# Two graph-attention layers on sparse neighbour lists: one release per tile, the last tiles of layer 0 placed earlier, another order of layer 1's tiles

## The chip, the cores and the metric

The kernel runs on one core of a Trainium2 chip, as one launch. The metric is the device time of that launch in microseconds; the median of several runs is given, and one further execution was taken with the profiler.

## What is computed

The input x is (8, 2048, 256), the adjacency matrix (2048, 2048) holds very few ones in a row. Cut to what matters:

```python
# layer 0: attention over the neighbours, a softmax in each chunk of 256 columns
scores = clip(einsum('bhnd,bhjcd->bhnjc', q, kc) / sqrt(Dh), -10, 10)
scores = where(mask == 0, -10, scores)
attn   = softmax(scores, axis=-1)
out    = einsum('bhnjc,bhjcd->bhnd', attn, vc) @ Wo.T + bo + x
x1     = layernorm(x + layernorm(out) * gamma + beta)
# layer 1: graph attention on x1, softmax over the neighbours
Wh     = x1 @ W
alpha  = softmax(where(mask, leaky_relu(s_src[:, :, None] + s_dst[:, None]), -inf), axis=2)
y      = layernorm(x1 + elu(einsum('bijh,bjhd->bihd', alpha, Wh)))
```

## The kernel before

**Tiles.** The kernel first turns the adjacency matrix into neighbour lists and sorts the 2048 nodes by their number of neighbours. 128 nodes make a tile, so there are 16 tiles, and `CAPS` (L34) gives the most neighbours that a node of each has: 24, 14, 13, 12, 11, 11, 10, 10, 9, 9, 8, 8, 7, 7, 6, 5. A "row" below is one neighbour of each of a tile's 128 nodes. The 8 batches are taken two at a time as four groups in layer 0 (`G` = 2, `NG` = 4) and four at a time as two halves in layer 1. Layer 0 therefore works through 4 x 16 = 64 tiles, layer 1 through 2 x 16 = 32.

**Gathers and the ring.** For each row, `gather` (L469) issues one indirect DMA on GpSimd's queue (L475), which fetches 128 table rows of 4 KB, from `kv_d` for layer 0 and from `wh_d` for layer 1. They land in a ring of 14 units of two rows each (`RING`, L39). A unit is free again once TensorE has summed its rows (`summed`, L500). VectorE multiplies the rows by weights beforehand (`weighted`, L487), and ScalarE does a part of them (L493). Before that, layer 0 multiplies by the queries (L533, L540), sums the products on TensorE (L552) and forms a softmax (L582 is its exponential); layer 1's softmax is in `softmax1` (L679 is its exponential).

**Layer 0's end of a tile.** `finish0` (L615) multiplies the context by Wo (L621), adds the input (L627), normalizes twice (L631 to L636), and stores the result in `x1_d`. `rows1` (L639) then multiplies that result by W (L649) and stores a block of 128 rows of `wh_d` (L653). A gather of layer 1 may read any row of its half's `wh_d`, so the first gather of a half needs the last block of that half.

**Layer 1's end of a tile.** `context1` (L689) ends with the load of `xr`, the tile's own rows of layer 0's result, on SP's queue (L711); `xr` has two buffers. `finish1` (L714) transposes the sums (L720), forms the ELU and adds `xr` (L724, L727), normalizes, and puts a scatter on the list `late`. The scatter goes out on GpSimd's queue. In the second half it writes four blocks straight to the output (L739), back in the nodes' own order. In the first half it writes to a table `hold_d` in that order (L734), and `release` (L760) later copies the held rows from there to the output, DRAM to DRAM, on SP's queue (L764), four transfers of 128 KB per tile.

**The order of the work.** It is written out by hand in `seq` (L750 to L758): groups 0 and 1 of layer 0 alone, then pairs of layer 0's tiles in groups 2 and 3 with one tile of layer 1's first half between the two of each pair, three pairs behind (`lag`), then layer 1's second half alone. `order` (L748) gives the tile for each place, for both layers alike: 15, 13, 11, ... 1, 0, 2, ... 14. In a pass of the loop, `fetch` (L777) first issues the gathers of the next place, then `scatters` sends what is in `late`. A tile of layer 1 that stands between two of layer 0 is only noted (`waiting`), and its context is formed in the next pass. The second half's passes, and those of the first half's last three tiles, run the last branch (L816 to L825): `softmax1`, `finish1` of the place before, from the third tile of the second half on one `release`, then `context1`. The two passes after layer 0's last tile also hold what is left of layer 0: `rows1` of tile 62 and `finish0` of tile 63 in the first, `rows1` of tile 63 in the second, in each case after `finish1` and before `context1`. A scheduler of the programming layer makes each engine's order out of this: it may move an instruction ahead of others of its engine where dependences allow.

Of the kernel before, what the change touches and what calls it, by code (L numbers as in the profile page):

```python
# [17 lines left out]
P = 128  # L18
# [15 lines left out]
CAPS = (24, 14, 13, 12, 11, 11, 10, 10, 9, 9, 8, 8, 7, 7, 6, 5)  # L34
TOP = 24
REC = 32
G = 2
# [134 lines left out]
def sparse_path(ctx: ExitStack, tc: tile.TileContext, keep, x, adj, Wq, bq, Wk, bk, Wv, bv, Wo, bo, gamma, beta, W, a,  # L172
                out):
    nc = tc.nc
    B, N, F = x.shape
    KC = F // P
    NT = N // P
    NCH = N // CH
    NG = B // G
# [13 lines left out]
    hold_d = [nc.dram_tensor(f"hold_d{p}", [N, 2 * GF], F32).ap() for p in range(NG // 2 - 1)]  # L193
# [313 lines left out]
    out_v = dram_disjoint_views(orows, 2 * NT * B)  # L507
# [150 lines left out]
    def fetch1(p, t):  # L658
        got1[p, t] = gather(2 * WW, wh_d[p], idx1, t)

    def softmax1(p, t):
        S = CAPS[t]
        units = got1[p, t]
        z = small.tile([P, 2, GH, S], F32, tag="z1", name="z1")
        for u, s0, n in units:
            nc.vector.tensor_tensor(z[:, :, :, s0:s0 + n].rearrange("p k e s -> p s k e"),
                                    u.rearrange("p s (k w) -> p s k w", k=2)[:, :, :, GF:GF + GH],
                                    sd[p % 2][:, t].unsqueeze(1).to_broadcast([P, n, 2, GH]), op=ALU.add)
        z = z.rearrange("p k e s -> p (k e) s")
        nc.vector.scalar_tensor_tensor(z, z, SLOPE, z, op0=ALU.mult, op1=ALU.max)  # L670

        neg = small.tile([P, S], F32, tag="neg", name="neg")
        nc.vector.tensor_scalar(neg, valid[:, t, 0:S], -1.0, 1e30, op0=ALU.add, op1=ALU.mult)
        nc.vector.tensor_tensor(z, z, neg.unsqueeze(1).to_broadcast([P, 2 * GH, S]), op=ALU.add)
        m = small.tile([P, 2 * GH], F32, tag="m", name="m")
        nc.vector.tensor_reduce(m, z, axis=AX.X, op=ALU.max)
        nc.vector.tensor_tensor(z, z, m.unsqueeze(2).to_broadcast([P, 2 * GH, S]), op=ALU.subtract)
        e = z
        nc.scalar.activation(e, z, AF.Exp)  # L679
        nc.vector.tensor_tensor(e, e, valid[:, t, 0:S].unsqueeze(1).to_broadcast([P, 2 * GH, S]), op=ALU.mult)  # L680
        r = small.tile([P, 2 * GH], F32, tag="r", name="r")
        nc.vector.tensor_reduce(r, e, axis=AX.X, op=ALU.add)

        nc.vector.tensor_scalar(r, r, 1e-30, None, op0=ALU.max)
        nc.vector.reciprocal(r, r)
        nc.vector.tensor_tensor(e, e, r.unsqueeze(2).to_broadcast([P, 2 * GH, S]), op=ALU.mult)  # L686
        st1[p, t] = e
# [61 lines left out]
    lag = 3  # L749
    seq = [(0, i) for i in range(2 * NT)]  # L750
# [6 lines left out]
            seq.append((0, 2 * NT + 2 * j + 1))  # L757
    seq += [(1, NT + j) for j in range(NT)]  # L758

    def release(p, t):  # L760

        for b in range(p * 2 * G, (p + 1) * 2 * G):
            c = b - p * 2 * G
            nc.sync.dma_start(out_v[NT * B + t * B + b][b * N + t * P:b * N + (t + 1) * P, :],  # L764
                              hold_d[p][t * P:(t + 1) * P, c * F:(c + 1) * F])

    def scatters():
        for f in late:
# [3 lines left out]
    def at(i):  # L772
        return i // NT, order[i % NT]

    fetched = [0]

    def fetch(k):  # L777

        while fetched[0] <= min(k, len(seq) - 1):
            layer, i = seq[fetched[0]]  # L780
            (fetch1 if layer else fetch0)(*at(i))
            fetched[0] += 1

    fetch(0)
    waiting = None
    for k, (layer, i) in enumerate(seq):
        g, t = at(i)
        between = layer == 0 and seq[k + 1][0] == 1
        tables_first = layer == 0 and seq[k + 1][0] == 0 and seq[k + 1][1] % NT == 0
        if not tables_first:  # L790
            fetch(k + 1)
        scatters()
        if layer == 0:
            scores0(g, t)
            if between and i + 1 < NG * NT:
                softmax1(*at(seq[k + 1][1]))
            if waiting is not None:

                if waiting:
                    finish1(*at(waiting - 1))  # L800
                context1(*at(waiting))
                waiting = None
            if i > 1:
                rows1(*at(i - 2))
            if i:
                finish0(*at(i - 1))
            if g + 1 < NG:
                tables(g + 1, i % NT)
            if tables_first:
                fetch(k + 1)  # L810
            softmax0(g, t)
            context0(g, t)
        elif seq[k - 1][0] == 0 and seq[k - 1][1] + 1 < NG * NT:
            waiting = i
        else:
            softmax1(g, t)  # L816
            finish1(*at(i - 1))
            if i >= NT + 2:
                release(g - 1, i - NT - 2)
            if seq[k - 1] == (0, NG * NT - 1):  # L820
                rows1(*at(NG * NT - 2))
                finish0(*at(NG * NT - 1))
            if seq[k - 2] == (0, NG * NT - 1):
                rows1(*at(NG * NT - 1))
            context1(g, t)  # L825
    scatters()
    finish1(*at(NG // 2 * NT - 1))
    scatters()
    for t in range(NT - 2, NT):
        for p in range(NG // 2 - 1):  # L830
# [429 lines left out]
```

## Time and profile before

| | |
|---|---|
| median of 6 runs | 2439.85 us |
| lowest and highest | 2431.14 and 2450.51 us |
| the profiled execution | 2445.62 us |
| its span, first to last instruction | 2443.9 us |
| PE, PEld busy | 1884.6 us (77%), 1615.9 us (66%) |
| DVE, ACT, POOL busy | 1843.0 us (75%), 1402.2 us (57%), 1479.3 us (61%) |
| gathers L475 from `kv_d` | 656, mean 1228 ns |
| gathers L475 from `wh_d` | 328, mean 1223 ns |
| releases on SP's queue | 64, 128 KB each, 8.2 us in the median from issue to landing |
| loads of `xr` | 32, 512 KB each, 5.2 us in the median from issue to landing |

PE is TensorE's matrix multiplication, PEld its loading of weights, DVE VectorE, ACT ScalarE, POOL GpSimd, SP SyncE, which here only issues DMAs. [...] The instructions that issue DMAs on SP are not counted as busy time; on POOL the indirect ones are. "L475" is a line of the kernel above. In a timeline, the bracket at the end of a line gives the time the engine stood idle before the instruction, and the event that came last before it started.

### The profile page before, as it was taken

Reading aid. Unit: us, or ns where it says so; the run is one execution under the profiler, and the core shown is the slowest. Engines: PE = TensorE matmul, PEld = TensorE weight load, DVE = VectorE, ACT = ScalarE, POOL = GpSimd, SP = SyncE. Lnnn points to the kernel's source line nnn. Section 1 sums busy time; section 2 is a strip of 40 time slices with the busy share of each in tenths; the row PEclk is TensorE's granted clock in tenths of the full one; section 3 lists DMA queues with packets and bytes.
Section 4 is the critical chain, followed back from the end, with each engine's and each line's share of the span. In section 5 each row is a group of like instructions: output and inputs, shape, how many; then the busy total and the mean of one; then the engine's idle time right before and its main releaser. Section 6 shows DMA issues by size and latency. Waiting matters only on the chain. (4 is left out here: it accounts for less than half of the span.)

```text
span 2443.9 us, 38937 instructions
## 1 busy us (share of the span) xinstructions
PE 1884.6 (77%) x11946; PEld 1615.9 (66%) x11946; DVE 1843.0 (75%) x4095; ACT 1402.2 (57%) x5031; POOL 1479.3 (61%) x1225
## 2 busy tenths in 40 slices
PE   6687787688988889999899997875767775455764
PEld 5565676577767778777788786764756664444653
DVE  4874467877767788867889887887879886656775
ACT  4573354355655566555566675666455577556766
POOL 1114644676545558376578757776778753758874
PEclk9998888889999999999999998987979987778887
DMA  6754886688888779598879979996779975986873
GB/s 218 253 189 142 299 286 224 223 305 321 284 290 289 260 239 378 206 362 310 285 265 346 354 259 337 325 305 231 232 234 328 363 271 173 379 286 228 288 277 109
DMA packets 240750, 669.11 MB, mean 274 GB/s; under 512 B 44455, under 2 KB 70826, under 8 KB 238486
## 3 DMA queue, kind: packets, MB, share of 16 engines
q0 software_dynamic: 156800, 505.01, 59.2%
q1 hardware_dynamic: 80016, 151.56, 17.0%
q10 hardware_dynamic: 3718, 9.97, 1.3%
q8 instruction: 98, 1.61, 0.3%
q14 instruction: 118, 0.97, 0.1%
HBM read 612.79 MB, written 126.36 MB: 302 GB/s over the span
## 5 line engine op out<-in xcount | busy, mean ns | idle before, releaser
L475 POOL DMA_INDIRECT u<-kv_d,idx x656 | 805.3, 1228 | 429.4 <-PE acc L500 165.1
L500 PE MATMUL acc<-ident,u 128*128 128x128 f32 x5248 | 726.1, 294 | 204.1 <-DVE u L487 130.1
L500 PEld LDWEIGHTS acc<-ident,u 128*128 128x128 f32 x5248 | 646.6, 153 | 268.8 <-DVE u L487 178.2
L475 POOL DMA_INDIRECT u<-wh_d,idx x328 | 401.3, 1223 | 155.6 <-issue 68.3
L552 PE MATMUL pr<-ident,u 128*128 128x128 f32 (+1 forms) x1984 | 283.9, 293 | 78.3 <-DVE u L533 63.4
L487 DVE TENSOR_TENSOR u<-u,al 128x1024 f32<-128x1024 f32 x280 | 332.5, 1221 | 1.3
L533 DVE TENSOR_TENSOR u<-u,qx 128x1024 f32<-128x1024 f32 (+1 forms) x248 | 295.3, 1191 | 27.7 <-DMA u<-kv_d,idx 24.5
L487 DVE TENSOR_TENSOR u<-u,z 128x1024 f32<-128x1024 f32 x266 | 315.1, 1213 | 0.8
L552 PEld LDWEIGHTS pr<-ident,u 128*128 128x128 f32 (+1 forms) x1984 | 244.0, 150 | 108.1 <-DVE u L533 86.1
L493 ACT ACTIVATE u<-u,z 128x64 f32<-128x64 f32 x1008 | 261.0, 336 | 27.8 <-DVE z L686 18.4
L493 ACT ACTIVATE u<-u,al 128x64 f32<-128x64 f32 x800 | 210.7, 342 | 42.4 <-DVE al L593 41.6
L348 POOL TENSOR_TENSOR xt<-xt,beta_r 128x1024 f32<-128x1024 f32 x32 | 80.1, 2507 | 186.1 <-PE tk L334 157.1
L382 PE MATMUL tk<-wq,xT 128*128 128x256 f32 x512 | 150.4, 410 | 44.6 <-ACT kvs L376 44.6
L649 PE MATMUL mf<-wa,x1T 128*128 128x264 f32 x512 | 157.8, 434 | 20.5 <-ACT x1T L644 10.5
L369 PE MATMUL tk<-wkv,xT 128*128 128x256 f32 x512 | 146.1, 399 | 14.9 <-ACT xC L339 14.7
L621 PE MATMUL mf<-wo,cT 128*128 128x256 f32 x512 | 143.8, 404 | 9.9 <-ACT whs L652 9.1
L540 DVE TENSOR_TENSOR u<-u,qx 128x1024 f32<-128x1024 f32 (+1 forms) x96 | 110.4, 1153 | 47.2 <-DMA qx<-qx_d,node 24.0
L373 PE MATMUL tk<-wkv,xC 128*128 128x256 f32 x512 | 143.5, 397 | 0.0
L649 PEld LDWEIGHTS mf<-wa,x1T 128*128 128x128 f32 x512 | 97.2, 207 | 54.8 <-ACT whs L652 23.0
L382 PEld LDWEIGHTS tk<-wq,xT 128*128 128x128 f32 x512 | 94.4, 205 | 58.5 <-ACT kvs L376 49.5
L441 ACT ACTIVATE sq<-o,nm 128x256 bf16<-128x256 f32 x256 | 129.4, 506 | 5.0
L437 ACT ACTIVATE nm<-sums 128x2 f32<-128x2 f32 (+1 forms) x160 | 32.4, 202 | 161.8 <-DVE sums L627 85.6
(166 smaller groups left out, 3160.7 us busy)
## 6 DMA issues: line engine op xcount, KB each, us to landing
kv_d<-kvs SPq DMA_DIRECT2D x48, 512.0 KB, 6.5
wh_d<-whs SPq DMA_DIRECT2D x64, 260.0 KB, 4.6
xt<-in_x_dram SPq DMA_DIRECT2D x64, 256.0 KB, 4.1
qx_d<-xt SPq DMA_DIRECT2D x32, 512.0 KB, 3.3
qx_d<-qs SPq DMA_DIRECT2D x64, 256.0 KB, 6.0
x_d<-o SPq DMA_DIRECT2D x64, 256.0 KB, 5.3
xr<-x_d SPq DMA_DIRECT2D x32, 512.0 KB, 5.2
u<-kv_d,idx POOLq DMA_INDIRECT x656, 6.3
```

The costliest lines, as they stand in the source:

```text
L369: nc.tensor.matmul(pm[:, 0:F], xT[:, b * KC + kc, rows], wkv[:, kc, 0:F], start=(kc == 0), stop=False, skip_group_check=True)
L373: nc.tensor.matmul(pm[:, F:], xC[:, b * KC + kc, rows], wkv[:, kc, F:], start=False, stop=(kc == KC - 1), skip_group_check=True)
L382: nc.tensor.matmul(qb, xT[:, b * KC + kc, rows], wq[:, kc, :], start=(b == 0 and kc == 0), stop=False, skip_group_check=True)
L441: nc.scalar.activation(sq, src[:, k, :], AF.Square, bias=nm[:, k:k + 1], accum_out=m2[:, k:k + 1])
L475: nc.gpsimd.indirect_dma_start(out=u[:, k, 0:width], out_offset=None, in_=table, in_offset=bass.IndirectOffsetOnAxis(ap=idx[:, t, s0 + k:s ...
L487: nc.vector.tensor_tensor(pv, pv, av, op=ALU.mult)
L493: nc.scalar.activation(pe, pe, AF.Copy, scale=al[:, e, s0 + k:s0 + k + 1])
L500: nc.tensor.matmul(acc[:, c, :], part[:, k, c * P:(c + 1) * P], ident, is_transpose=True, start=first and k == 0 and c == 0, stop=last and ...
L533: nc.vector.tensor_tensor(prod.rearrange("p k j (s w) -> p k j s w", w=W8), u[:, :, 0:GF].rearrange("p s (k j w) -> p k j s w", k=UNIT, w=W8),
L552: nc.tensor.matmul(pr[0:n * W8, k, :], prod[:, j // (NJ // UNIT), j % (NJ // UNIT), :], ident, is_transpose=True, start=(j == 0), stop=(j ...
L621: nc.tensor.matmul(po[:, b, :], cT[:, b * KC + kc, :], wo[:, kc, :], start=(b == 0 and kc == 0), stop=False, skip_group_check=True)
L649: nc.tensor.matmul(pw[:, 0:F + 2 * H], xT[:, b * KC + kc, :], wa[:, kc, :], start=(kc == 0), stop=(kc == KC - 1))
```

## The change

It touches the order of the work in three places. No arithmetic is changed.

First, `release` makes one transfer of 512 KB per tile out of four, with the four batches as a dimension of it, and pins it to its place in SP's program order. It is called after `context1` of the same pass, and so after that pass's load of `xr`.

Second, in the pass after layer 0's last tile, `rows1` of tile 62 and `finish0` of tile 63 stand ahead of `softmax1`, and `rows1` of tile 63 stands right after it, in the same pass and ahead of `finish1` and `context1`.

Third, layer 1's first half gets an order of its own, `order1`. `beside(j)` adds up the caps of the pair of layer 0's tiles that follows around place j. The places with the smallest sums get the tiles in the order 1, 2, 3, 0, 4, 5, ... 15. The caps of the 16 places were 5, 7, 8, 9, 10, 11, 12, 14, 24, 13, 11, 10, 9, 8, 7, 6, and become 7, 6, 9, 10, 11, 24, 10, 8, 7, 5, 8, 9, 11, 14, 13, 12. The order of layer 0 and that of layer 1's second half stay.

```diff
+    def beside(j):
+        return sum(CAPS[order[i % NT]] for i in (2 * (j + lag), 2 * (j + lag) + 1) if i < 2 * NT)
+    order1 = [0] * NT
+    for j, t in zip(sorted(range(NT), key=beside), list(range(1, lag + 1)) + [0] + list(range(lag + 1, NT))):
+        order1[j] = t
+
     def release(p, t):
 
-        for b in range(p * 2 * G, (p + 1) * 2 * G):
-            c = b - p * 2 * G
-            nc.sync.dma_start(out_v[NT * B + t * B + b][b * N + t * P:b * N + (t + 1) * P, :],
-                              hold_d[p][t * P:(t + 1) * P, c * F:(c + 1) * F])
+
+        b0, rows = p * 2 * G, slice(t * P, (t + 1) * P)
+        tc.keep_in_program_order(nc.sync.dma_start(
+            out_v[NT * B + t * B + b0].rearrange("(b n) f -> n b f", b=B)[rows, b0:b0 + 2 * G, :],
+            hold_d[p][rows, :].rearrange("n (b f) -> n b f", f=F)))
...
+    def at1(i):
+        return i // NT, order[i % NT] if i >= NT else order1[i]
+
...
             layer, i = seq[fetched[0]]
-            (fetch1 if layer else fetch0)(*at(i))
+            (fetch1(*at1(i)) if layer else fetch0(*at(i)))
...
         else:
+
+            last = seq[k - 1] == (0, NG * NT - 1)
+            if last:
+                rows1(*at(NG * NT - 2))
+                finish0(*at(NG * NT - 1))
             softmax1(g, t)
-            finish1(*at(i - 1))
+            if last:
+                rows1(*at(NG * NT - 1))
+            finish1(*at1(i - 1))
+            context1(g, t)
             if i >= NT + 2:
                 release(g - 1, i - NT - 2)
-            if seq[k - 1] == (0, NG * NT - 1):
-                rows1(*at(NG * NT - 2))
-                finish0(*at(NG * NT - 1))
-            if seq[k - 2] == (0, NG * NT - 1):
-                rows1(*at(NG * NT - 1))
-            context1(g, t)
     scatters()
-    finish1(*at(NG // 2 * NT - 1))
+    finish1(*at1(NG // 2 * NT - 1))
```

The other calls of `softmax1`, `finish1` and `context1` take their tile from `at1` in the same way.

More of the change, by code (lines that the diff above doesn't have):

```diff
@@ L786, in sparse_path @@
     for k, (layer, i) in enumerate(seq):
-        g, t = at(i)
+        g, t = at1(i) if layer else at(i)
         between = layer == 0 and seq[k + 1][0] == 1
@@ L795, in sparse_path @@
             if between and i + 1 < NG * NT:
-                softmax1(*at(seq[k + 1][1]))
+                softmax1(*at1(seq[k + 1][1]))
             if waiting is not None:
                 if waiting:
-                    finish1(*at(waiting - 1))
-                context1(*at(waiting))
+                    finish1(*at1(waiting - 1))
+                context1(*at1(waiting))
                 waiting = None
```

## The prediction

> **What bounds the kernel now.** I read the windows by stage first, to see which engine each stage leaves no room. Columns: stretch and its length, busy us of PE, PEld, DVE, ACT, POOL, then granted clock, DMA share and GB/s. The stages are groups 2 and 3 of layer 0 beside the first half of layer 1 (the part with group 3), the seam where layer 0 ends, and the second half of layer 1 in three parts.
>
> ```profile
> 1483.00:1993.00 510.00, 372.10 (x2484) 324.79 (x2485) 419.38 (x888) 295.14 (x1096) 371.72 (x294) 0.87 0.85 297
> 1993.00:2051.00 58.00, 44.44 (x284) 37.95 (x282) 44.19 (x132) 45.57 (x168) 12.08 (x9) 0.88 0.33 119
> 2051.00:2167.00 116.00, 47.23 (x290) 42.34 (x289) 62.04 (x168) 57.64 (x189) 79.23 (x70) 0.67 0.97 352
> 2167.00:2396.00 229.00, 152.23 (x1038) 131.40 (x1036) 172.72 (x393) 162.51 (x584) 182.35 (x148) 0.83 0.75 262
> ```
>
> Between two POOL instructions the timeline shows 0.3 us of issue. So POOL is occupied for 371.7 + 0.3 x 294 = 460 of 510 us in the first stage and for 182.4 + 0.3 x 148 = 227 of 229 us in the last. GpSimd, which issues one gather per row of a tile, sets the pace there; DVE (82% and 75%) is next. In the two stages between it does not, and the timelines of POOL and SP say why (start, length, what, and in brackets the idle time before):
>
> ```profile
> 2006.41 1.22 POOL L475 DMA_INDIRECT u<-wh_d,idx  x1 [0.30 <-issue]
> 2022.41 1.96 POOL L734 DMA_INDIRECT hold_d<-xr,node  x1 [14.78 <-DVE u L487]
> 2046.56 0.96 POOL L734 DMA_INDIRECT hold_d<-xr,node  x1 [22.18 <-ACT xr L456]
> 2051.53 1.02 POOL L475 DMA_INDIRECT u<-wh_d,idx  x1 [4.01 <-PE mf L720]
> ```
>
> The gather at 2051.53 is the first from the second half's table. It needs the last row block of that table, whose store SP issues at 2048.43. From 2007.6 POOL gathers nothing for 44 us, and PE then waits 11.05 us for its first rows (2067.47).
>
> ```profile
> 2048.43 0.32 SPq L653 DMA_DIRECT2D wh_d<-whs  x1
> 2050.00 37.10 SPq L711 DMA_DIRECT2D xr<-x_d  x3
> 2087.14 34.09 SPq L764 DMA_DIRECT2D out_dram<-hold_d  x30
> 2122.36 0.33 SPq L711 DMA_DIRECT2D xr<-x_d  x1
> 2123.32 35.78 SPq L764 DMA_DIRECT2D out_dram<-hold_d  x33
> 2160.24 0.33 SPq L711 DMA_DIRECT2D xr<-x_d  x1
> ```
>
> Two loads of xr stand behind 30 and 33 releases, about 1.1 us each. Both are waited for:
>
> ```profile
> 2128.91 0.69 DVE L724 SCALAR_TENSOR_TENSOR xr<-mf,xr 128x512 f32<-128x512 f32 x1 [16.77 <-DMA u<-wh_d,idx]
> 2164.98 0.69 DVE L724 SCALAR_TENSOR_TENSOR xr<-mf,xr 128x512 f32<-128x512 f32 x1 [17.38 <-DMA xr<-x_d]
> ```
>
> The first names a gather, but it is the instruction that takes xr, and it starts 6.5 us after that load's issue; I read it as the same wait. DVE loses 34 us. POOL, running ahead through the ring, loses less:
>
> ```profile
> 2167.54 0.98 POOL L475 DMA_INDIRECT u<-wh_d,idx  x1 [13.66 <-PE acc L500]
> 2171.69 1.53 POOL L475 DMA_INDIRECT u<-wh_d,idx  x1 [1.44 <-PE acc L500]
> ```
>
> Less 0.3 us of issue each, and with 0.3 and 1.6 at 2120 and 2141, that is 16 us.
>
> [...] SP's own waits are on L711 (249.7 us for scatters of xr), and everything behind it stands. [...] The trace: 30 issues of 128 KB took 34.09 us, while single loads of 512 KB issue in 0.32. [...] from 1290 us on, gathers whose first 0.99 us met none of the large DVE multiplies (L487, L533, L540) took 1.01 us (221 of them), those fully beside one 1.67 us (161). So a busier DVE makes POOL's work longer.
>
> **Part 1, release.** 64 transfers of 128 KB become 16 of 512 KB, pinned in SP's program order after the load of xr. In the built program each load of xr from the third of the second half on is followed by one release, the last by three. Bytes are the same: the trace has 8,192 packets of 1,024 bytes for them at 47.5 ns, 24.3 us of all 16 engines, now 1.5 us per tile instead of all in 2087 to 2161. A tile lasts about 20 us and its stretch has a DMA share of 0.75, so I cost the transfer at nothing; the cover is gone only if a release needs over some 15 us, while in the burst it got through in 73 / 16 = 4.6 us. A release [...] stands ahead of the next xr alone, which is issued a tile later. The last three fall after the last xr, 17 us before the last scatter (2418.1 and 2434.8 now), with 5 us of transfer: hidden. Removed: POOL's 16 us, DVE's 34. POOL's is the one that counts, since POOL paces what follows: -16, between -16 and -34.
>
> **Part 2, the last tiles of layer 0.** In the built program the finishing of tile 63 and its rows (L621, L649) stand on PE before layer 1's tile 14 (numbers are places in its sequence from 0), where before the last rows came among tile 15. That chain, from the finishing of tile 62 (L627, 2003.3) over its rows (2022.5), the finishing of 63 (2027.4 to 2042.1), its rows and store (2048.4) to the first gather at 2051.5, is 48 us of steps that each need the one before. I keep 48; it could be 40 (less beside it) or 56 (engines wait in order for it). No instruction is added; tile 13's multiplies cover the first half of the chain, tile 14's the second. If that cover fails, DVE idles up to 20 us, but POOL has a full ring meanwhile. What is late next is the ring: at the chain's end tiles 14 and 15 hold 7 and 6 of its 14 units, so the gathers of the second half go as those are consumed (25 rows, some 40 us, against 28 rows or 43 us of gathering). I take 8 us lost, between 0 and 25. The built program also puts six gathers of the second half, which wait for the table, ahead of the scatter of tile 12 on POOL, and the xr load of tile 14 waits for that scatter: within those 8.
>
> **Part 3, order of the first half.** Same tiles, same rows. Caps in order, before: 5 7 8 9 10 | 11 12 14 24 13 11 10 9 | 8 7 6; after: 7 6 9 10 11 | 24 10 8 7 5 8 9 11 | 14 13 12, with bars at the start of group 3 and at the end of layer 0. Up to layer 0's end 143 rows become 125: 18 fewer. What is a row worth there? From the exponentials of layer 0's tiles (L582) at 1538.6, 1597.8, 1665.5, 1852.0, 1913.6 and 1962.4, stretches with 29, 35, 100, 32 and 27 rows (pair and layer 1 tile) took 59.2, 67.7, 186.5, 61.6 and 48.8 us: 1.8 us a row. POOL gives the same: (1.26 + 0.3) / 0.9 = 1.73. So the chain starts 18 x 1.73 = 31 us earlier (23 at the bare 1.3 us per gather, 35 at 1.93). The 18 rows are not saved, they move beside and behind the chain, where POOL idled for 44 us. Evening out the heaviest stretch gets nothing: its 100 rows already took 1.87 us each. The tile of 24 now comes right after POOL's gap of 23.44 us at 1462.17: its softmax needs all 24 gathers, 13 more than before, 20 us of waiting for DVE but not for POOL. Cost 0, up to 20.
>
> **Sum**, against the profiled execution (2445.62 us; span 2443.9): the second half starts 31 us earlier, -31; POOL's stalls, -16; ring at the seam, +8; DVE busier beside POOL, +5 (its share in 2051 to 2396 goes from 0.68 to some 0.73, a tenth more of the 46 us that POOL's 218 instructions there took over 0.99 each; 0 to 10). Together -34: 2412. The median of the runs, 2439.85, lies 6 us below that execution; there it gives 2406.
>
> **Rivals.** (a) Only the release counts: the chain stretches to 56 us and the ring takes 25, so 31 is given back; 2440 - 16 + 5 = 2429. For it: POOL must wait for consumption of 13 units. Against: in 1483 to 1993 the ring keeps POOL 90% occupied. (b) DVE, not POOL, paces the second half: then both stalls count in full, -34, beside the -31, and neither ring nor contention takes anything back: 2440 - 65 = 2375. Against: POOL's 227 of 229 us. (c) Slower: the tile of 24 at the start of group 3. With 12 of 14 units it stands in front of the next tile of layer 0 just when the ring is empty. The consumers wait 20 us more, and if POOL then waits until it is consumed (24 rows at 1.2 us of L487, 29 us), 49 us go, and the consumers pace group 3, so that 18 rows are worth 22 us, not 31: 2440 + 49 - 22 - 16 + 5 + 8 = 2464. It decides from 25 us of loss on. Against: before, the same tile followed 12 and preceded 14 and 24 rows without visible cost. (d) The change not doing what it says: the built program shows the moves on SP and PE, so no weight.
>
> **Chances.** Forecast 0.54, own range 2390 to 2422; (a) 0.19; (b) 0.14; (c) 0.13. No change is within 0.5% (12 us, about what a measurement of this kernel can tell): 2428 to 2452. (a) lies on that edge, half to each side: faster 0.54 + 0.14 + 0.09 = 0.77, same 0.10 and 0.02 of (c), slower 0.11. The range leaves out (c) and the far end of (b): 2378 to 2432.
>
> **What would show it.** Right: no L724 waiting over 5 us for xr; SP with one release after each xr; first gather from the second table near 2020 us; no gap of POOL over 5 us from there to the last gathers. Wrong: a POOL gap before the gathers that follow the tile of 24 (z of 128x384, about 1520), a seam gap that stays 40 us, or gathers of the second half over 1.35 us in the mean.

## The result, and the profile after

The changed kernel takes 2431.68 us in the median of 37 runs (2417.79 to 2451.63), the kernel before 2443.67 us in 74 runs beside them: ratio 0.9957, 95% interval 0.9943 to 0.9971, or some 10.5 us of the 34 that I forecast. The profiled execution took 2439.78 us, its span 2438.1. (Ratios in this document leave out runs over 1.5% above a kernel's fastest; in the first eight experiments that cuts into the ordinary spread, so the medians of all runs stand beside them.)

The windows of the changed kernel at the seam, now 1984 to 2037 where it was 1993 to 2051, and behind it, with the columns of the prediction:

```profile
1984.00:2037.00 53.00, 36.08 (x217) 30.27 (x215) 44.65 (x105) 36.95 (x143) 32.96 (x27) 0.80 0.78 281
2037.00:2152.00 115.00, 76.72 (x513) 67.55 (x512) 82.48 (x233) 84.24 (x288) 78.89 (x67) 0.80 0.77 273
```

At the seam POOL now works 33 us instead of 12. DVE works as before (44.65 us, before 44.19) and PE less (36.08, before 44.44). The rows are gathered earlier and not consumed earlier. POOL and SP of the changed kernel around the first gather of the second half:

```profile
2023.17 0.99 POOL L475 DMA_INDIRECT u<-wh_d,idx  x1 [0.30 <-issue]
2036.57 1.05 POOL L475 DMA_INDIRECT u<-wh_d,idx  x1 [12.41 <-issue]
...
2044.52 0.99 POOL L475 DMA_INDIRECT u<-wh_d,idx  x1 [5.60 <-PE acc L500]
```

```profile
2054.93 60.16 SPq L711 DMA_DIRECT2D xr<-x_d  x5
2115.15 0.66 SPq L771 DMA_DIRECT2D out_dram<-hold_d  x1
2129.39 0.34 SPq L711 DMA_DIRECT2D xr<-x_d  x1
2129.78 0.55 SPq L771 DMA_DIRECT2D out_dram<-hold_d  x1
```

The gather at 2036.57 is the second half's first: 15 us earlier than before (2051.53), not 31, and 12.2 us earlier when both executions are counted from the same point of layer 0 (A in the table below). Of POOL's gap of 44 us there are 12.41 and 5.60 left. At the second POOL waits for PE's sums (L500): the ring is full. One release follows each load of xr, in 0.66 and 0.55 us of issue where four took some 4.5 in the burst before (34.09 us for 30). The two waits for xr on DVE are gone:

```profile
2124.04 0.69 DVE L724 SCALAR_TENSOR_TENSOR xr<-mf,xr 128x512 f32<-128x512 f32 x1
...
2143.12 0.68 DVE L724 SCALAR_TENSOR_TENSOR xr<-mf,xr 128x512 f32<-128x512 f32 x1
```

So each move is visible, and two thirds of the gain are missing. From its first gather to its last the second half took 347.1 us; before, with both stalls in it, 338.6.

### The profile page after: what moved, and what is told of

Read it like the earlier page. It is cut to its first block, busy times and chain, and to the rows that moved or that the text cites. A ratio compares the mean times of both kernels' runs of the same rounds, so it can differ in the third digit from the quotient of the medians.

```text
span 2438.1 us, 38848 instructions
## 1 busy us (share of the span) xinstructions
PE 1897.2 (78%) x11946; PEld 1620.2 (66%) x11946; DVE 1842.6 (76%) x4095; ACT 1404.5 (58%) x5031; POOL 1481.1 (61%) x1225
## 5 line engine op out<-in xcount | busy, mean ns | idle before, releaser
L500 PE MATMUL acc<-ident,u 128*128 128x128 f32 x5248 | 711.9, 291 | 157.9 <-DVE u L487 97.4
L500 PEld LDWEIGHTS acc<-ident,u 128*128 128x128 f32 x5248 | 634.2, 151 | 222.9 <-DVE u L487 145.6
L475 POOL DMA_INDIRECT u<-wh_d,idx x328 | 408.7, 1246 | 146.6 <-issue 73.1
L649 PE MATMUL mf<-wa,x1T 128*128 128x264 f32 x512 | 167.6, 454 | 22.8 <-ACT x1T L644 12.9
L649 PEld LDWEIGHTS mf<-wa,x1T 128*128 128x128 f32 x512 | 101.7, 217 | 60.4 <-ACT whs L652 23.4
```

The source lines that it names most:

```text
L475: nc.gpsimd.indirect_dma_start(out=u[:, k, 0:width], out_offset=None, in_=table, in_offset=bass.IndirectOffsetOnAxis(ap=idx[:, t, s0 + k:s ...
L500: nc.tensor.matmul(acc[:, c, :], part[:, k, c * P:(c + 1) * P], ident, is_transpose=True, start=first and k == 0 and c == 0, stop=last and ...
L649: nc.tensor.matmul(pw[:, 0:F + 2 * H], xT[:, b * KC + kc, :], wa[:, kc, :], start=(kc == 0), stop=(kc == KC - 1))
```

## Experiments

**How they are compared.** Three lengths come from each trace. A runs from the exponential (L582) of layer 0's 32nd tile, ahead of which the kernels hardly differ while single executions do by up to 24 us, to the first gather of layer 1's second half. B runs from there to the last gather. The rest is 54 to 55 us in each. A and B come from one execution of each kernel. The changed kernel and e12 are alike up to the first gather of the second half, yet A is 1013.8 and 1006.8 us, so I read nothing into single differences of up to 7 us. "Open" counts, at the first gather of the second half, the matmuls L500 (sums of rows, 8 per row) and L720 (finish, 8 per tile) of the first half that have not run. Rows are those of layer 1's first half ahead of layer 0's end. Ratios are to the kernel before, on chips where that takes 2432 to 2444 us.

| kernel | rows | A | B | A + B | L500, L720 open | ratio, interval |
|---|---|---|---|---|---|---|
| before | 143 | 1026.0 | 338.6 | 1364.6 | 0, 8 | |
| release (e14) | 143 | 1023.0 | 322.0 | 1345.0 | 0, 8 | 0.9914 (0.9877 to 0.9951) |
| release, four transfers (e18) | 143 | 1022.0 | 324.6 | 1346.6 | 0, 8 | 0.9951 (0.9924 to 0.9978) |
| release, last tiles (e15) | 143 | 1022.5 | 346.6 | 1369.1 | 104, 26 | 1.0015 (0.9991 to 1.0039) |
| same, milder (e17) | 143 | 1018.5 | 333.4 | 1351.9 | 48, 18 | 0.9981 (0.9963 to 1.0000) |
| release, sequence (e16) | 125 | 1007.4 | 337.7 | 1345.1 | 160, 16 | 0.9929 (0.9907 to 0.9951) |
| all three: the changed kernel | 125 | 1013.8 | 347.1 | 1360.9 | 200, 26 | 0.9957 (0.9943 to 0.9971) |
| last tiles, sequence (e12) | 125 | 1006.8 | 351.1 | 1357.9 | 200, 26 | 0.9983 (0.9967 to 1.0000) |
| all, large tiles last (e9) | 113 | 1009.7 | 336.1 | 1345.8 | 195, 16 | 0.9919 (0.9888 to 0.9949) |
| e9 without last tiles ahead (e13) | 113 | 1015.1 | 334.6 | 1349.7 | 148, 16 | 0.9937 (0.9900 to 0.9975) |

In the first eight runs, taken in two groups, every kernel took some 9% longer (before: 2656.78 us for e1 to e4, 2657.93 for e5 to e8) with twice the spread. They decided little; e1, e4 and e5 were repeated as e14, e15 and e16.

**e1, the release alone** (`release` itself as in the change).

```diff
         finish1(*at(i - 1))
-        if i >= NT + 2:
-            release(g - 1, i - NT - 2)
...
         context1(g, t)
+        if i >= NT + 2:
+            release(g - 1, i - NT - 2)
```

> The kernel before with the new release alone (one transfer of 512 KB per tile, behind the load of xr). Theory A (the release is worth what POOL lost to the late loads, about 12 to 16 us, and the rest of the change nets to nothing or less): 2443 - 14 = 2429, ratio 0.993 to 0.995, so as fast as the whole change. Theory B (DVE's 34 us count in full, since DVE and POOL both wait for the same tile; the change gives back 20 elsewhere): 2409, ratio 0.986. Theory C (the gain comes from the earlier start of the second half alone, the removed stalls are only moved to another wait): 2440 to 2445, ratio 0.999 to 1.001.

Ratio 0.9979 (0.9952 to 1.0006), median 2648.64. Too wide to tell A from C; B (0.986) is excluded.

**e2, the last tiles of layer 0 ahead, alone.**

```diff
+        if last:
+            rows1(*at(NG * NT - 2))
+            finish0(*at(NG * NT - 1))
         softmax1(g, t)
+        if last:
+            rows1(*at(NG * NT - 1))
         finish1(*at(i - 1))
...
-        if seq[k - 1] == (0, NG * NT - 1):
-            rows1(*at(NG * NT - 2))
-            finish0(*at(NG * NT - 1))
-        if seq[k - 2] == (0, NG * NT - 1):
-            rows1(*at(NG * NT - 1))
         context1(g, t)
```

> The kernel before with the last tiles of layer 0 ahead of layer 1's work at the seam alone. The chain from tile 62's finishing to the first gather of the second half was 48 us before and 44 after. Theory A (the seam's later loss of some 20 us comes with the 14, 13 and 12 row tiles of the other order): 4 us earlier start and no loss, -2 to -6, ratio 0.998 to 0.999. Theory B (the loss comes with this part, because six gathers of the second half stand ahead of a scatter to the held rows on POOL): +8 to +16, ratio 1.003 to 1.007. The two late loads of xr stay, so nothing of the release shows here.

Ratio 1.0042 (1.0015 to 1.0069), median 2667.78: 11 us slower. Theory B's size: a loss comes with this part even with the old sequence.

**e3, the sequence alone** (`order1` and `at1` in the kernel before).

```diff
-        g, t = at(i)
+        g, t = at1(i) if layer else at(i)
```

> The kernel before with the own sequence of layer 1's first-half tiles alone. My prediction: 31 us earlier end of layer 0 and 8 back at the seam, -23, ratio 0.991. Theory A (the tile of 24 rows right after the gap of group 3, a late load of x in group 2, and large tiles at the seam take it back): layer 0 ends about 9 us earlier, the seam costs 10 to 20 more, total 0 to +8, ratio 1.000 to 1.003. Theory B (the seam's loss is not its own): -9, ratio 0.996.

Ratio 0.9986 (0.9959 to 1.0014), median 2652.16. The forecast's 23 us are excluded; the two theories are not told apart.

**e4, release and last tiles, old sequence.**

```diff
         order1[j] = t
+    order1 = order
```

> The changed kernel without its own sequence for layer 1's first half (the old sequence is kept; new release and last tiles ahead stay). Theory A (the sequence gives back what it brings): -16 to -20 against before, ratio 0.992 to 0.9935, so 6 to 10 us faster than the changed kernel. My prediction's sums without the 31 us: -16 + 5 = -11 and a few us of the chain, ratio 0.994 to 0.9955, near the changed kernel. If the sequence is worth 20 us or more as forecast, this is slower than the changed kernel by that: ratio above 1.000.

Ratio 1.0048 (1.0018 to 1.0079), median 2661.61: slower than the kernel before, by what e2 loses. Theory A, that the sequence gives back what it brings, doesn't explain that.

**e5, release and sequence, last tiles where they were.**

```diff
-        if last:
-            rows1(*at(NG * NT - 2))
-            finish0(*at(NG * NT - 1))
         softmax1(g, t)
-        if last:
-            rows1(*at(NG * NT - 1))
         finish1(*at1(i - 1))
+        if seq[k - 1] == (0, NG * NT - 1):
+            rows1(*at(NG * NT - 2))
+            finish0(*at(NG * NT - 1))
+        if seq[k - 2] == (0, NG * NT - 1):
+            rows1(*at(NG * NT - 1))
         context1(g, t)
```

> The changed kernel with the last tiles of layer 0 left where they were (new release and own sequence stay). The two runs with the last tiles ahead were slower than those without by 0.4 to 0.7%, and from the first gather of the second half to its last they took 354 and 359 us against 341. Theory P (putting the last tiles ahead holds the finish of layer 1's tile before the seam back behind the whole chain on PE, so its scatter, the two xr tiles and all that waits for them come late): 8 to 16 us faster than the changed kernel, ratio to before 0.989 to 0.9925; its second half takes 330 to 338 us. Theory S (the tiles of 14, 13 and 12 rows at the seam make the lockstep): no faster than the changed kernel, ratio 0.995 to 0.998.

Ratio 1.0013 (0.9971 to 1.0055), median 2650.41 against 2657.93. Inconclusive here; see e16.

**e6, the changed kernel with the finish of layer 1's tile 12 in front.**

```diff
         if last:
+            finish1(*at1(i - 1))
             rows1(*at(NG * NT - 2))
             finish0(*at(NG * NT - 1))
         softmax1(g, t)
+        if not last:
+            finish1(*at1(i - 1))
+        context1(g, t)
         if last:
             rows1(*at(NG * NT - 1))
-        finish1(*at1(i - 1))
-        context1(g, t)
```

> The changed kernel with one step moved back: the finish of layer 1's tile before the seam stands ahead of layer 0's last tiles again, which still stand ahead of the other layer 1 work; the last rows follow the context of the tile. Theory P (it is that finish, held back, that costs): 8 to 16 us faster than the changed kernel, ratio to before 0.989 to 0.9925, no wait over 5 us for a scatter to the held rows in the 60 us after the first gather. Theory P2 (it is the chain's place ahead of layer 1's multiplies that costs): as the changed kernel, within 4 us. Theory S (large tiles at the seam): as the changed kernel.

Ratio 0.9982 (0.9946 to 1.0018), median 2643.09, three us below e8. Theory P in its narrow form, that only this finish counts, gets no support.

**e7, the tile of 24 rows one place later.**

```diff
         order1[j] = t
+    order1[5], order1[6] = order1[6], order1[5]
```

> The changed kernel with the tile of 24 rows one place later (places 5 and 6 of the sequence exchanged, so a tile of 10 rows follows the gap at the start of group 3). My rival (c): the tile of 24 at the empty ring costs; the measured loss there against before is about 14 us of softmax time, of which part came back later: layer 0's end 5 to 14 us earlier, ratio to the changed kernel 0.994 to 0.998. If what came later had to be waited for anyway (its 24 rows stand somewhere in group 3): no difference, 0.999 to 1.001.

Ratio 1.0039 (1.0002 to 1.0076), median 2660.35: not faster. Its one trace has layer 0's end 20 us earlier after the 32nd tile than that of e8 (1059.4 and 1079.6 us), so trace and times disagree. Open.

**e8, the changed kernel again.** No edit.

> The changed kernel once more, beside the three others on their chip. All theories: ratio to before 0.9957 as first measured (0.994 to 0.997). On a chip on which all runs take 9% longer the parts might count differently; if the removed stalls are hidden by longer waits there, 0.998 to 1.003.

Ratio 0.9980 (0.9948 to 1.0012), medians 2646.19 and 2657.93 (0.9956): as first measured.

**e9, the three largest tiles last.** 113 rows stand ahead of layer 0's end.

```diff
         order1[j] = t
+    free = list(range(NT))
+    for j, c in enumerate((7, 6, 9, 10, 11, 12, 10, 8, 7, 5, 8, 9, 11, 24, 14, 13)):
+        order1[j] = next(t for t in free if CAPS[t] == c)
+        free.remove(order1[j])
```

> The changed kernel with the three largest tiles (24, 14, 13 rows) as the last three of layer 1's first half, a tile of 12 in the place that the 24 had: 113 rows stand before layer 0's end, where the changed kernel has 125 and the kernel before 143. The rule of my prediction (1.73 us for each row that is moved past layer 0's end, filled in where POOL idles): 12 rows, 21 us faster than the changed kernel, ratio to before 0.987 to 0.989. Theory C (DVE, PE and ACT need the time for these rows wherever they stand, so that a row moved is a row owed): layer 0 ends 15 to 20 us earlier and the tiles after the seam come that much later than they would, within 5 us of the changed kernel, ratio 0.994 to 0.998.

Ratio 0.9919 (0.9888 to 0.9949), 2415.72 against 2432.39 us: by the ratios 9 us under the changed kernel where the rule gives 21, and the two intervals still touch. Layer 0 ends 925.2 us after its 32nd tile instead of 960.9, but the first gather comes only 4 us sooner (A): of the 51 rows that now stand behind layer 0's last tiles POOL has 36 still to gather, and it waits 23.4 us for ring space among them.

**e10, the three smallest last.** The same lines with the caps 14, 13, 9, 10, 11, 24, 10, 8, 7, 12, 8, 9, 11, 7, 6, 5.

```diff
+    for j, c in enumerate((14, 13, 9, 10, 11, 24, 10, 8, 7, 12, 8, 9, 11, 7, 6, 5)):
```

> The changed kernel with the three smallest tiles (7, 6, 5 rows) last in layer 1's first half and 14, 13 and 12 rows in their places: 146 rows stand before layer 0's end, 21 more than in the changed kernel. The rule of my prediction: 36 us slower than the changed kernel, ratio to before 1.010 to 1.012. Theory C (a row moved is a row owed): within 5 us of the changed kernel, ratio 0.994 to 0.998. In between, if the small tiles at the seam leave PE without cover while it waits for the last tiles' steps (about 12 us of waiting where the old sequence had tiles of 8, 7 and 6 there): 10 to 15 us slower, ratio 1.000 to 1.002.

Ratio 1.0062 (1.0023 to 1.0101), 2451.85 us: between the theories. From e10 to e9 are 33 rows and 36 us. I first took that for a price of 1.1 us a row. It is not one: e10 also has small tiles behind the last tiles of layer 0, which costs by itself (e15), and in e13 no gain is left for the rows.

**e11, three buffers for xr.**

```diff
-        qx = work.tile([P, 2 * GF], F32, tag="qx", name="qx", bufs=4)
+        qx = work.tile([P, 2 * GF], F32, tag="qx", name="qx", bufs=3)
...
-        xr = work.tile([P, 2, GF], F32, tag="xr", name="xr")
+        xr = work.tile([P, 2, GF], F32, tag="xr", name="xr", bufs=3)
```

> The changed kernel with three tiles of xr instead of two; the buffers of qx go from four to three to make room. At the seam the loads of xr wait for the scatters of two tiles before, and POOL's scatters for the tiles that use xr. Theory X (this lockstep took about 15 of the 20 us that the tiles after the seam lost): 10 to 18 us faster than the changed kernel, ratio to before 0.988 to 0.992, no wait of over 3 us for a scatter in the 60 us after the first gather of the second half. Theory C (the consumers need the time anyhow): within 5 us of the changed kernel. A loss of more than 5 us would be the missing buffer of qx in layer 0.

Ratio 1.0180 (1.0133 to 1.0227), 2478.28 us. Most of the loss is qx's: the 32nd tile of layer 0 came at 1052.8 us instead of 1022.8, with POOL waiting 80.5 us for the missing buffer. From there to the end it took 1416.1 us, the changed kernel 1415.3, and B is 343.4 us against 347.1. Theory X's 10 to 18 us do not show. The missing buffer still counts in this stretch (POOL waits 24.8 us for qx behind L633 there, 13.4 in the changed kernel), so a smaller gain is not excluded.

**e12, the changed kernel with the old release** (`release` as in the kernel before).

```diff
-        context1(g, t)
         if i >= NT + 2:
             release(g - 1, i - NT - 2)
+        context1(g, t)
```

> The changed kernel with the old release: four transfers per tile, free to stand where the scheduler puts them; last tiles ahead and own sequence stay. It shows what the release is worth in the changed kernel. My prediction: 16 us slower than the changed kernel, ratio to before 1.001 to 1.003. If DVE's two waits count in full: 34 us slower, 1.008 to 1.011. If the late loads of xr only take the place of other waits: within 4 us of the changed kernel, 0.994 to 0.998.

Ratio 0.9983 (0.9967 to 1.0000), 2428.62 against 2432.39 us. Inside the changed kernel the release is worth 0.26%, 6 us, by intervals that just touch; B is 4.0 us longer without it. The trace of e12 says why. These are the two L724 that take late loads of xr, though neither line names the load:

```profile
2119.45 0.69 DVE L724 SCALAR_TENSOR_TENSOR xr<-mf,xr 128x512 f32<-128x512 f32 x1 [5.00 <-DMA u<-wh_d,idx]
...
2144.25 0.69 DVE L724 SCALAR_TENSOR_TENSOR xr<-mf,xr 128x512 f32<-128x512 f32 x1 [7.44 <-DMA out_dram<-xr,nodeb]
```

In the kernel before the waits were 16.77 and 17.38 us. By then the second half is late for another reason, and the same lateness is not paid twice.

The next four ran on one chip (before: 2433.07 us).

**e13, e9 with the last tiles of layer 0 where they were** (the edit of e5 on e9).

```diff
-        if last:
-            rows1(*at(NG * NT - 2))
-            finish0(*at(NG * NT - 1))
...
+        if seq[k - 1] == (0, NG * NT - 1):
+            rows1(*at(NG * NT - 2))
+            finish0(*at(NG * NT - 1))
...
```

> The sequence with 24, 14 and 13 rows last, with the new release, but with the last tiles of layer 0 left where the kernel before has them. Together with the changed kernel and the three others it tells what putting the last tiles ahead is worth when large tiles follow, and when small ones do. Theory D (rows moved behind layer 0's end pay only if the last tiles stand ahead of them, since otherwise the large tile's multiplies lie in front of the last rows on PE and DVE): 10 to 15 us slower than with the last tiles ahead, ratio to before 0.997 to 0.999. Theory L (putting them ahead costs 12 to 15 us whatever follows): 12 to 15 us faster than that, ratio 0.986 to 0.988.

Ratio 0.9937 (0.9900 to 0.9975), 2421.70 us: between the two theories, and like e9 within the intervals. With large tiles behind them no cost of the last tiles' place shows, though these intervals of 0.3 to 0.4% each way could hide one of 10 us.

**e14, the release alone, again** (the edit of e1, cut here).

```diff
...
+        if i >= NT + 2:
+            release(g - 1, i - NT - 2)
```

> The kernel before with the new release alone, again, beside the next two on one chip. Theory A (POOL's stalls count, 12 to 16 us): ratio 0.993 to 0.995. Small (what the first run of it and the changed kernel with the old release show, 6 to 8 us): 0.9965 to 0.9975.

Ratio 0.9914 (0.9877 to 0.9951), 2416.63 us: -16.4. That is theory A's mechanism, a little more than its range (0.993 to 0.995, which the interval reaches into), and more than the whole change brings. B falls from 338.6 to 322.0 us, and at the right place: counted from the first gather, the sixth tile starts after 71.1 us before and 73.3 here, the eighth, behind the two stalls, after 132.2 and 118.9, the last after 330.2 and 313.5 (first gather of each). In B of e14, and of e18 below, POOL never stands for more than half a microsecond between two instructions (in e14 257.08 us busy with 214 of them and 65.0 between them, 0.30 each), so there the second half is as short as POOL's own work.

**e15, release and last tiles, again** (the edit of e4).

```diff
+    order1 = order
```

> New release and last tiles ahead with the old sequence, again. Theory D (with tiles of 8, 7 and 6 rows at the seam PE stands still for some 12 us between the last tiles' steps, and layer 1's tiles are late by that): 10 to 18 us slower than the release alone, ratio 1.000 to 1.004. If the last tiles ahead bring the 4 us by which their chain is shorter: 0.993 to 0.996.

Ratio 1.0015 (0.9991 to 1.0039), 2438.55 us: 22 us slower than e14 on the same chip. Theory D, and the traces show it. First PE in e14 (start, length, what), from the last steps of finishing tile 63 to its rows:

```profile
2017.62 0.38 PE L311 MATMUL mf<-ident,bO 128*128 128x128 f32 x2
2017.84 1.80 PE L500 MATMUL acc<-ident,u 128*128 128x128 f32 x15
...
2020.05 3.11 PE L500 MATMUL acc<-ident,u 128*128 128x128 f32 x27
...
2029.34 2.84 PE L500 MATMUL acc<-ident,u 128*128 128x128 f32 x24 [1.23 <-ACT hT L708]
2032.23 0.44 PE L305 MATMUL tf<-ident,o 128*128 128x128 f32 x2
...
2033.84 1.16 PE L649 MATMUL mf<-wa,x1T 128*128 128x264 f32 x4
```

Then the same steps in e15:

```profile
2015.07 0.63 PE L311 MATMUL mf<-ident,bO 128*128 128x128 f32 x2
2027.64 1.18 PE L305 MATMUL tf<-ident,o 128*128 128x128 f32 x4 [11.94 <-ACT o L456]
2029.49 2.13 PE L649 MATMUL mf<-wa,x1T 128*128 128x264 f32 x4 [0.68 <-ACT x1T L644]
```

In e14 PE sums layer 1's rows while DVE and ACT normalize tile 63. In e15 the same sums stand behind the last rows in PE's own order, and PE waits 11.94 us. DVE has done the multiplies (15 of them start within the chain in both), so the 13 rows of layer 1's last two tiles lie in the ring, weighted and not summed: 13 x 8 = 104 L500 open, and the finish of three tiles (24 L720, and 2 of a fourth). Their scatters stand among the second half's gathers on POOL. The last three of e14, then of e15 (first gathers 2041.25 and 2037.83):

```profile
2036.28 0.96 POOL L734 DMA_INDIRECT hold_d<-xr,node  x1 [18.91 <-ACT xr L456]
2056.87 1.19 POOL L734 DMA_INDIRECT hold_d<-xr,node  x1 [0.30 <-DMA u<-wh_d,idx]
2070.82 1.30 POOL L734 DMA_INDIRECT hold_d<-xr,node  x1 [0.30 <-ACT u L493]
```

```profile
2056.66 1.15 POOL L734 DMA_INDIRECT hold_d<-xr,node  x1 [1.52 <-ACT xr L456]
2078.77 1.02 POOL L734 DMA_INDIRECT hold_d<-xr,node  x1 [10.55 <-ACT nm L437]
2089.65 1.24 POOL L734 DMA_INDIRECT hold_d<-xr,node  x1 [1.43 <-ACT xr L456]
```

The last comes 29.6 us after the first gather in e14 and 51.8 us in e15. The difference of 22 us is about the loss; it is nearly complete by the fifth tile of the second half (first gather 51.5 and 72.1 us after the half's first). B as a whole, in e14 and then in e15:

```profile
2041.25:2363.30 322.05, 195.16 (x1310) 170.95 (x1311) 234.55 (x554) 215.23 (x760) 257.08 (x214) 0.78 0.82 299
2037.83:2384.45 346.62, 216.22 (x1442) 187.71 (x1440) 240.03 (x586) 228.50 (x801) 261.48 (x215) 0.78 0.78 283
```

POOL's busy time grows by 4.4 us, and the time in which it stands from 65.0 to 85.1: these 20 us are waits for data of scatters. PE's granted clock is 0.78 in both, so the clock is not what makes B longer.

**e16, release and sequence, again** (the edit of e5, cut here).

```diff
-        if last:
-            rows1(*at(NG * NT - 2))
-            finish0(*at(NG * NT - 1))
...
```

> New release and own sequence with the last tiles of layer 0 left where they were, again. The changed kernel has ratio 0.9957. Theory D (sequence and last tiles bring something only together): as the release alone, 0.996 to 0.998. Theory L (putting the last tiles ahead costs whatever follows): 12 to 15 us faster than the changed kernel, 0.989 to 0.991. The rule of my prediction corrected to 1.1 us a row, with nothing lost: 18 rows, 20 us, and 7 for the release: 0.989.

Ratio 0.9929 (0.9907 to 0.9951), 2412.32 us: between the ranges of D and L, and like e14 within the intervals, as D has it. The sequence brings the first gather 15.6 us forward (A, 1023.0 to 1007.4) and B grows by 15.7: 20 rows, 160 L500, are open at that gather. A row moved is a row owed. B of e16:

```profile
2015.90:2353.60 337.70, 221.00 (x1478) 190.74 (x1479) 251.81 (x590) 232.68 (x831) 264.72 (x215) 0.80 0.79 288
```

Against e14 POOL is busy for 7.6 us more and stands for 8.0 more (73.0 us). The last tiles ahead, added to this, take the ratio to 0.9957, another 0.3% or some 7 us. The intervals of the two overlap and they were not measured together, so the times alone do not show this loss; nor do e5 and e8, which were measured together (1.0013 and 0.9980, with wide intervals). The traces agree with it: B is 9.4 us longer in the changed kernel, of which POOL stands for 8.7.

**e17, the last tiles ahead in a milder form, old sequence** (the edits of e6 and e4 together).

```diff
+    order1 = order
...
         if last:
+            finish1(*at1(i - 1))
             rows1(*at(NG * NT - 2))
...
```

> New release, old sequence, and the last tiles ahead in a milder form: the finish of layer 1's tile 12 stands in front of them, and the last rows follow the context of tile 13. In the built order on PE 54 of layer 1's accumulating matmuls (L500) then stand between the finish of tile 63 and its last rows, where release and last tiles alone have none and the release alone has 86 and more. Theory D (what is lost is layer 1's work that is not done under the chain: 104 matmuls and the finish of two tiles outstanding at the first gather of the second half cost 22 us): about 50 outstanding, some 8 to 12 us slower than the release alone, ratio to before 0.995 to 0.998. If any such work behind the last rows costs the whole: 1.000 to 1.003. If only the finish of tile 12 counts: as the release alone, 0.990 to 0.993.

Ratio 0.9981 (0.9963 to 1.0000), 2439.88 against 2444.03 us. 48 L500 are open instead of 104, B is 333.4 us: 11.4 above e14, where e15 is 24.6 above. POOL stands for 71.8 us in B, where it was 65.0 and 85.1. About half the work held back, about half the loss in B; in the times it is 9 us against e18, measured beside it, and 16 by the ratios against e14, so the ratio lies at the edge of theory D's range.

**e18, four transfers, but behind the load of xr.**

```diff
-            nc.sync.dma_start(out_v[NT * B + t * B + b][b * N + t * P:b * N + (t + 1) * P, :],
-                              hold_d[p][t * P:(t + 1) * P, c * F:(c + 1) * F])
+            tc.keep_in_program_order(nc.sync.dma_start(
+                out_v[NT * B + t * B + b][b * N + t * P:b * N + (t + 1) * P, :],
+                hold_d[p][t * P:(t + 1) * P, c * F:(c + 1) * F]))
...
-        if i >= NT + 2:
-            release(g - 1, i - NT - 2)
...
         context1(g, t)
+        if i >= NT + 2:
+            release(g - 1, i - NT - 2)
```

> The release in four transfers of 128 KB as before, but pinned in program order behind the load of xr, old sequence and last tiles where they were: place without size. Four issues take about 4.4 us on SP per tile, which is ahead of nothing but the next load of xr, a tile of some 20 us later. Theory place: as the release in one transfer, ratio 0.990 to 0.994. Theory size (the number of transfers counts): 0.996 to 1.000.

Ratio 0.9951 (0.9924 to 0.9978), 2430.97 against 2444.03 us, between the two ranges; but B is 324.6, so 14.0 of the 16.6 us that one transfer gains in B are there. SP of e18:

```profile
2124.85 0.33 SPq L711 DMA_DIRECT2D xr<-x_d  x1
2125.23 2.57 SPq L764 DMA_DIRECT2D out_dram<-hold_d  x4
```

Place is most of it. Four issues of 128 KB took 2.4 to 3.3 us here, and up to 2300 SP's next load of xr came 8.7 to 37.8 us behind them. The intervals of e14 and e18 overlap, so whether the size adds anything is not shown.

**Versions that look better than both.** The release alone (2416.63 against 2433.07 us), release and sequence (2412.32 against 2433.07) and e9 (2415.72 against 2432.39) beat the kernel before clear of noise, by 0.7 to 0.9%. Their intervals overlap with each other and still touch that of the changed kernel, which was not measured beside them, so that they beat it too is likely and not shown. The release alone is the smallest edit.

## Why the prediction was wrong in size

**The release, -16: right.** -16.4 us in the times and -16.6 in B, when done alone. POOL's stalls were the measure, not DVE's 34 us. In the changed kernel it is worth 6, since the waits it removes had shrunk to 5.00 and 7.44 us there (e12). I added the parts up as if they were independent.

**"The chain starts 18 x 1.73 = 31 us earlier": the step that failed.** A is 1006.8 to 1013.8 us in the three kernels with this sequence (e16, e12, the changed kernel) and 1022.0 to 1026.0 in the kernel before, e14 and e18: the second half starts some 14 us earlier, not 31 (15.6 from e14 to e16). Already at layer 0's end little has been won: in e16 it comes 954.0 us after the 32nd tile instead of 967.5, 0.75 us a row. The five stretches that I read gave 1.8 to 2.0 us a row (1.9 in the mean), but the average price of a stretch is not what it gains by losing a row. With another 12 rows fewer and no tile of 24 rows in group 3 layer 0's end comes 22.7 us earlier (e13 against e16, 1.9 us a row) or 35.7 (e9 against the changed kernel, 3.0). So the tile of 24 in group 3 is a likely cause of the poor price; but e7, which moved it by one place, wasn't faster, and this stays open.

An earlier end of layer 0 is not yet a gain, either, because a row moved behind layer 0's end has still to be gathered, multiplied and summed. My own first view had the warning in its second line: in those 58 us POOL worked for 12.08, but DVE for 44.19 and PE for 44.44. POOL had time, the engines that consume its rows had a quarter of it. With the new release and the last tiles where they were, A + B is 1345.0, 1345.1 and 1349.7 us for 143, 125 and 113 rows ahead (e14, e16, e13). In the times e16 differs from e14 by +0.15% with some 0.4% to either side, which excludes the 18 us that I forecast for the sequence, 31 less 13.

**The ring at the seam, +8, and DVE beside POOL, +5: right in sum.** The sequence's part of B is +15.7 (e14 to e16), near the 13 of both terms, and it cancels the 15.6 us that the sequence brings. POOL stands for 8.0 us more, but at scatters and not for ring space, so the ring was not the wait there. POOL's gathers took 1252 ns in the mean against 1222 in e14, 4.9 us over the 164 of the half (1226 in the changed kernel); that DVE beside them is the reason was not tested.

**"I keep 48 ... No instruction is added", a cost of nothing: failed too.** The chain, from the finishing of tile 62 to the first gather, took 43.4 us in the changed kernel, but it took 44.6 in e14 and 44.0 in e16 too, where the last tiles stand as before: the new place did not shorten it. And what I named as its cover, layer 1's multiplies, is DVE's work. PE's part of the same tiles, the sums and the finish, went behind the chain, and I did not ask who waits for that. It costs 22 us with small tiles at the seam (e15) and, as far as the changed kernel and e16 can be compared, about 7 with those of 14, 13 and 12 rows, where 58 L500 still stand under the last steps of the chain. I looked for late work on POOL, and the order that changed was PE's.

**Put together.** Release -16, sequence 0, last tiles +7: -9 against -10.5 measured. These are steps on the way from the kernel before over e14 and e16 to the changed kernel, so their ratios add up by construction; what this tests is that separate measurements agree. Of the 24 us missing some 15 are the 31, 3 the terms against it and 7 the last tiles. Rival (a), in which only the release counts and the 31 us are given back, named 2429, and the time is 2431.68. That is in part luck: its chain of 56 us did not come, the chain took 43.4; what the sequence brought was given back all the same, and the last tiles, which it has at nothing, took some 7. Rival (b), DVE's stalls in full, falls with e14. Rival (c) is not shown: POOL's gap at the start of group 3 is 24.13 us after 23.44 before, and no loss of 25 us follows.

## What to carry to other kernels

Before a row moved into the idle time of the engine that feeds a ring is counted as saved, read all engines of that window: here POOL worked for 12.08 of 58 us, but DVE for 44.19 and PE for 44.44, and the 18 rows moved there left A + B where it was (1345.0 us in e14, 1345.1 in e16). When a latency chain is put ahead, list per engine what now stands behind it, by instruction and not by tile: in e15 the multiplies were under the chain, while 104 sums and the finish of three tiles, in PE's order, were not, and e15 took 22 us more than e14. And measure each part alone before the sum is trusted: the release gained 16.4 us alone and 6 in the changed kernel, where the waits it removes were already shorter.

## What the runs showed that I had not expected

The matmuls of the chain put ahead ran at half the clock in e15: granted 0.50, where e14 has 1.00. Windows of e15 up to the end of the chain, then of e14 over its wait (after the five busy times: granted clock of PE, DMA share, GB/s):

```profile
2004.00:2016.00 12.00, 9.84 (x24) 6.00 (x23) 7.23 (x13) 5.55 (x24) 0.00 (x0) 0.50 0.11 44
2016.00:2028.00 12.00, 0.36 (x2) 0.29 (x2) 9.78 (x27) 8.53 (x32) 0.00 (x0) 0.50 0.00 1
2028.00:2038.00 10.00, 6.73 (x19) 3.89 (x18) 1.26 (x4) 2.26 (x9) 0.17 (x1) 0.50 0.14 53
```

```profile
2016.00:2028.00 12.00, 10.10 (x82) 9.06 (x80) 12.00 (x28) 11.73 (x47) 1.37 (x1) 1.00 0.29 112
```

Four matmuls of the last rows (L649) take 2.13 us in e15, without layer 1's sums beside them, and 1.16 in e14. What sets the granted clock to half these runs do not show: in e15 the window from 1996 to 2004 has 0.95 in the mean and the one from 2004 on 0.50. Ahead of 2003.78 PE was idle for 2.61 us, the longest stretch since 1985, and the clock stays at 0.50 to 2016 while PE is busy for 9.84 of 12 us. The chain as a whole was hardly longer for it: from the finishing of tile 62 to the first gather 45.5 us in e15 and 44.6 in e14, from the finishing of tile 63 to its last rows 16.5 and 17.8. So a cost of the half clock to the kernel does not show in these runs.

In the first eight runs, where everything took 9% longer, the waits view shows PE standing for nothing that the profile shows in 130 places for 213 us (e8), against 7 places and 52 us for the same kernel in the result's own trace. Why is not known. The record gives e5 to e8 (before: 2657.93 us) and e17 and e18 (2444.03) the same chip number, so it need not be the chip.
